# Spreads of 1/std on 32 rows of the array, in pairs, and paired second projection products

## The chip, the cores and the metric

The kernel runs on one core of one Trainium2 chip. The metric is the device time of one execution in microseconds. The engines are named as in the profile: PE is TensorE's matmul, PEld its loading of weights, DVE is VectorE, ACT is ScalarE, POOL is GpSimd, and SP, ACT and POOL issue DMAs. [...]

## The reference, cut to what matters

Four images of 96 channels and 64 x 64 pixels go through four residual layers: a bidirectional two-dimensional state space layer, a deformable convolution, a layer of Fourier mixing with a quantized feed-forward network, and linear attention with a second quantized feed-forward network. Two pieces matter here. The first is the layer normalization over channels, which stands ahead of the first layer, of the Fourier mixing, of the attention and of both feed-forward networks:

```python
def _ln_t(v, eps=1e-5):
    m = jnp.mean(v, axis=-1, keepdims=True)
    s = jnp.var(v, axis=-1, keepdims=True)
    return (v - m) / jnp.sqrt(s + eps)
```

The second is the projection ahead of the state space scan. It is taken over the pixels in row order and in column order (both also backwards):

```python
x0 = xc.reshape(Bsz, Di, L)
x1 = jnp.transpose(xc, (0, 1, 3, 2)).reshape(Bsz, Di, L)
x_hwwh = jnp.stack([x0, x1], axis=1)
xs = jnp.concatenate([x_hwwh, jnp.flip(x_hwwh, axis=-1)], axis=1)
x_dbl = jnp.einsum('bkdl,kcd->bkcl', xs, x_proj_w)
```

`Di` is 192, so each projection contracts over 128 + 64 channels.

## The kernel before, in words

**Layout.** Channels lie on partitions and pixels along the free dimension. An image of 4096 pixels is cut into 8 chunks of 512, the width of one PSUM bank.

**Norms.** `centred` multiplies each chunk by a centring matrix, squares the result on ScalarE, and sums the squares of all chunks of a norm into one bank: chunk j lands in the 32 partitions 32 (j % 4) and following, in row j // 4 of them. `inv_sqrt_steps` makes 1/std of that bank, one tile `rstd` of 128 x 512, in which the row 32 (j % 4) + j // 4 holds chunk j. To multiply a chunk by its 1/std, the row has to stand on all channel partitions. `spread` (line 523) does that: a matmul with `rstd` as the moving operand and one column of the identity, repeated 128 times, as weights. It writes one bank, `lnb` in the profile (`lnbf` in the feed-forward networks, `lnbo` in the output norm of the first layer). VectorE then multiplies the chunk by it (line 734 in the first layer, line 1613 in `normed`).

**Projection.** `projected` makes, for chunk j and each order q in `qs`, one bank `px`: first a product over 128 channels (line 812), then one over the last 64 (line 814), whose inputs lie on partitions 0 to 63 for row order and 64 to 127 for column order. ScalarE evicts the bank with a bias (line 815). Image 0 is projected one order at a time (`first`), images 1 to 3 with both orders in one call (`before`).

**The scan.** 1536 units of 128 x 1024 each. For each, ScalarE makes the decay (`da`, line 1014), TensorE spreads the inflow into two banks (`db`, line 1020), VectorE multiplies it (line 1034) and runs the recurrence (`hh`, line 1042), GpSimd weighs the states (line 1051), and TensorE sums them (`py`, line 1070). This is the frame of the kernel.

**Side work.** All else is two streams of Python generators that are stepped between the units: `ends` (image 0's start, the starts of images 1 to 3, then the last layers of each image) and `middle` (the output of the first layer and the deformable convolution of each image). A step issues a few instructions and yields their estimated cost. `pipe` runs several chains of steps at once and takes the next step that the planner's clock has room for. Every engine then runs its instructions in program order. After the last scan the side streams run alone; image 3's last layers run as two halves of the image.

**Banks.** While the scans run, both streams share three banks. `has_bank` tells whether one is free, by the count of banks held; a step says with `holds` how many its chain holds after it, and with `new` that the next step takes a new one. After the scans the `ends` stream, and the first half of image 3, has five banks of its own; the other stream keeps the three.

What the code before does at the places of the change:

```python
def chain(j):
    cs = slice(j * CH, (j + 1) * CH)
    pb = net.spread(rs, 32 * (j % 4) + groups.index(j // 4), C, key)
    yield cost(pe=1.2, holds=1)
    net.nc.vector.tensor_mul(tl[:C, cs], tl[:C, cs], pb)
    yield cost(dve=0.7)
```

Of the kernel before, what the change touches and what calls it, by code (L numbers as in the profile page):

```python
# [8 lines left out]
F32 = mybir.dt.float32  # L9
# [5 lines left out]
AF = mybir.ActivationFunctionType  # L15
# [4 lines left out]
B, C, H, W = 4, 96, 64, 64  # L20
# [5 lines left out]
CH = 512  # L26
NCH = L // CH
NR = CH // W
# [7 lines left out]
NX = 64 + R + 1 + 2 * NS  # L36
# [146 lines left out]
def cost(pe=0.0, dve=0.0, act=0.0, pool=0.0, **more):  # L183
    return Step((pe, dve, act, pool), **more)


def wait(us=0.0, **more):

    return Step((0.0,) * 4, us, **more)
# [82 lines left out]
def pipe(net, chains, width, every=0, lane=None, **tiles):  # L272


    chains, active = iter(chains), []
    clock, known, more = net.clock, net.known, True
    end, free = clock.now(), tiles
    while True:
        if more and len(active) < width:
            steps = next(chains, None)  # L280
            if steps is None:
                more = False
            else:
                active.append(Chain(steps, clock.now()))
                continue
        if not active:
            break
        for n, chain in enumerate(active):
            if chain.new and not net.has_bank():
                continue  # L290
            if any(
                a.done <= chain.done + every
                for a in active[:n]
                if lane is None or (a.kind is lane) == (chain.kind is lane)
            ):
                continue
            if not all(free[tag] > 0 for tag in chain.takes):
                continue
            if clock.has_room(known.get((chain.kind, chain.done), (1.0,) * 4), chain.ready):
                break  # L300
        else:
            yield BLOCKED
            continue
        for tag in chain.takes:
            free[tag] -= 1
        clock.precede(known.get((chain.kind, chain.done), (0.0,) * 4))
        step = next(chain.steps, None)
        if step is None:
            net.hold(-chain.holds)
            active.remove(chain)  # L310
            end = max(end, chain.ready)
            continue
        for tag in step.frees:
            free[tag] += 1
        known[chain.kind, chain.done] = step.work
        chain.ready = clock.queue(step, chain.ready)
        chain.done += 1
        net.hold(step.holds - chain.holds)
        chain.holds, chain.new, chain.takes = step.holds, step.new, step.takes
        yield None  # L320
    yield wait(max(0.0, end - clock.now()))
# [38 lines left out]
class Net:  # L360
# [39 lines left out]
        own = self.own_banks and self.stream.own  # L400
        return (self.own_banks if own else self.psum).tile([128, CH], F32, name=name, tag="mm")[:p]

    def has_bank(self):
        if self.own_banks:
            return self.stream.held < (5 if self.stream.own else 3)
        return sum(stream.held for stream in self.streams) < 3

    def hold(self, n):
        self.stream.held += n
# [63 lines left out]
    def centred(self, x, cen, dst, key, pool, bias=None, groups=(0, 1)):  # L473
# [36 lines left out]
        def chains():  # L510
            for r in groups:
                for q in range(4):
                    yield chain(4 * r + q)
                yield sums(r)

        yield from pipe(self, chains(), 5, every=-99, sq=4, v0=-3, v1=-3)
        rstd = pool.tile([128, CH], F32, name=f"lns{key}", tag="lns", bufs=1)
        nw = pool.tile([128, CH], F32, name=f"lnw{key}", tag="lnw", bufs=1)
# [4 lines left out]
    def spread(self, rstd, j, n, key):  # L523

        pb = self.mm(f"lnb{key}_{j}")
        row = self.ident[:, j : j + 1].to_broadcast([128, 128])
        self.nc.tensor.matmul(pb, lhsT=row, rhs=rstd, start=True, stop=True)
        return pb[:n]


# [24 lines left out]
class Layer0:  # L555
# [54 lines left out]
    def first(self):  # L610
# [5 lines left out]
        with tc.tile_pool(name=f"l0u{b}", bufs=1) as up, tc.tile_pool(name=f"l0b{b}", bufs=1) as sm:  # L616
# [25 lines left out]
            def columns():  # L642
                for j in range(NCH):
                    yield self.projected(b, j, us, xp_a, xp_c, sm, xdbl, (1,))
                    for ks in ((1,), (1, 3), (3,)):
                        yield self.steps(b, ks, j, us, dtw, sm, xdbl)

            yield from pipe(net, columns(), 5, every=2, ex=3, lw=2, rl=2, du=2)

    def before(self, b):  # L650
# [22 lines left out]
    @staticmethod  # L673
    def rows(pad, j):
        return pad[:, 1 + j * NR : 1 + (j + 1) * NR, 1 : 1 + W]

    @staticmethod
    def as_rows(t):
        return t.rearrange("p (h w) -> p h w", w=W)
# [25 lines left out]
    def normed_rows(self, b, x, pad):  # L705

        net, rows, as_rows = self.net, self.rows, self.as_rows
        tc, nc = net.tc, net.nc
        with tc.tile_pool(name=f"l0n{b}", bufs=2) as sm:
            for edge in (pad[:, 0, :], pad[:, PW - 1, :], pad[:, :, 0], pad[:, :, PW - 1]):  # L710
                nc.gpsimd.memset(edge, 0.0)
            yield wait(4.0)
            stats = []
            yield from net.group_norm_stats(x, sm, f"0_{b}", stats)
            mean, rstd = stats

            cen = sm.tile([C, 128], F32, name=f"cen{b}", tag="cen", bufs=1)
            nc.vector.tensor_scalar_mul(cen, net.cen96, rstd)
            yield cost(dve=0.3)
            net.hold(1)  # L720
            pb = net.mm(f"cb{b}")
            nc.tensor.matmul(pb[:, 0:1], lhsT=cen, rhs=mean, start=True, stop=True)
            bias = sm.tile([C, 1], F32, name=f"cenb{b}", tag="cenb", bufs=1)
            nc.scalar.mul(bias, pb[:C, 0:1], -1.0)
            net.hold(-1)
            yield cost(pe=0.3, act=0.3)

            rs = yield from net.centred(x, cen, lambda j: (rows(pad, j), as_rows), f"0_{b}", sm, bias)

            def chain(j):  # L730
                pb = net.spread(rs, 32 * (j % 4) + j // 4, C, f"0_{b}")
                yield cost(pe=1.2, holds=1)
                r = rows(pad, j)
                nc.vector.tensor_mul(r, r, as_rows(pb))
                yield cost(dve=0.7)
                nc.scalar.activation(r, r, AF.Identity, scale=net.vec(V_ING, C), bias=net.vec(V_INB, C))
                yield cost(act=0.8)

            yield from pipe(self.net, (chain(j) for j in range(NCH)), 3)

    def conv_weights(self, b, sm):

# [56 lines left out]
    def projected(self, b, j, us, xp_a, xp_c, sm, xdbl, qs, takes=""):  # L799


        net = self.net
        nc = net.nc
        cs = slice(j * CH, (j + 1) * CH)
        if takes:
            yield wait(new=True, takes=takes)
        for q in qs:
            xd = sm.tile([NX, CH], F32, name=f"xd{b}_{q}_{j}", tag=f"xd{q}")
            hp = slice(64 * q, 64 * q + 64)
            ua = us[0][:, cs] if q == 0 else us[1][:, j * NR : (j + 1) * NR, :]  # L810
            px = net.mm(f"px{b}_{q}_{j}")
            nc.tensor.matmul(px, lhsT=xp_a[:, q, :], rhs=ua, start=True, stop=False)
            yield cost(pe=1.3, holds=1)
            nc.tensor.matmul(px, lhsT=xp_c[hp], rhs=us[2][hp, cs], start=False, stop=True)
            nc.scalar.activation(xd, px[:NX], AF.Identity, bias=net.vec(V_X1, NX))
            xdbl[q, j] = xd
            yield cost(pe=1.3, act=0.7, new=q == 1 and len(qs) > 1)
        for q in qs:
            nc.sync.dma_start(self.bc_d[b][q][:, cs], xdbl[q, j][: 2 * NS])
            nc.sync.dma_start(self.bc_d[b][q + 2][:, cs], xdbl[q, j][64 + R + 1 :])  # L820
        yield NOTHING
# [781 lines left out]
def normed(net, t, tl, key, pool, groups=(0, 1)):  # L1603

    rs = yield from net.centred(
        t, net.cen96, lambda j: (tl[:C, j * CH : (j + 1) * CH], plain), key, pool, groups=groups
    )

    def chain(j):
        cs = slice(j * CH, (j + 1) * CH)  # L1610
        pb = net.spread(rs, 32 * (j % 4) + groups.index(j // 4), C, key)
        yield cost(pe=1.2, holds=1)
        net.nc.vector.tensor_mul(tl[:C, cs], tl[:C, cs], pb)
        yield cost(dve=0.7)

    yield from pipe(net, (chain(j) for j in chunks(groups)), 3)


def chunks(groups):
    return [4 * r + q for r in groups for q in range(4)]  # L1620


class Ffn:
# [23 lines left out]
    def run(self, b, t, groups=(0, 1), side="left"):  # L1647
# [3 lines left out]
        with (  # L1651
            tc.tile_pool(name=f"fb{n}_{b}", bufs=1, side=side) as big,
            tc.tile_pool(name=f"fs{n}_{b}", bufs=2, side=side) as pool,
        ):
            tl = big.tile([C, L], F32, name=f"fl{n}_{b}", tag="tl")
            yield from normed(net, t, tl, f"f{n}_{b}", pool, groups)

            def chunk(j):
# [49 lines left out]
class LinearAttention:  # L1708
# [8 lines left out]
    def run(self, b, t, groups=(0, 1), side="left", shared=None):  # L1717
# [3 lines left out]
        with (  # L1721
# [3 lines left out]
            tl = big.tile([C + 1, L], F32, name=f"tl3{key}", tag="tl")  # L1725
            nc.gpsimd.memset(tl[C:], 1.0)
            yield from normed(net, t, tl, f"3_{key}", pool, groups)
            net.hold(1)
            pa = net.mm(f"pa{key}", C)[:, :C]
# [191 lines left out]
```

## Time and profile before

| what | us |
|---|---|
| median of three runs | 8629.55 |
| lowest and highest of them | 8617.16, 8655.84 |
| the profiled execution, its own time | 8600.48 |
| its span, first to last instruction | 8598.7 |
| PE busy | 6553.4 |
| DVE busy | 6817.9 |
| ACT busy | 4945.4 |
| POOL busy | 5626.7 |

Durations are read from the one profiled execution. A busy TensorE is not TensorE at its peak, since matmuls are pipelined and their ends are modelled. An fp32 matmul shows as two matmul instructions, each with its own weight load. The groups that the change touches, from the page's list by line and engine (busy time, mean of one in ns, then the engine's idle time before them and what ended it):

```profile
L527 PE MATMUL lnb<-lns,w_ident 128*128 128x512 f32 x192 | 114.0, 726 | 23.4 <-DVE lns L436 14.2 <-issue 4.1 <-DVE tl L1613 3.6
L527 PE MATMUL lnbf<-lnsf,w_ident 128*128 128x512 f32 x128 | 74.4, 708 | 22.2 <-DVE lnsf L436 13.0 <-DVE fl L1613 9.2
L527 PE MATMUL lnbo<-rs,w_ident 128*128 128x512 f32 x64 | 51.4, 918 | 23.4 <-DVE rs L436 11.0 <-DVE cc L1173 5.0 <-DVE rl L853 4.4
L812 PE MATMUL px<-xa,w_xp_a 128*128 128x512 f32 x128 | 109.4, 947 | 41.1 <-DVE rl L853 24.8 <-DMA w_xp_a<-in_xp_a 8.9 <-ACT zt L789 7.0
L814 PE MATMUL px<-xc,w_xp_c 64*128 64x512 f32 x128 | 90.0, 790 | 0.0
```

### The profile page before, as it was taken

How to read it: one execution, taken by the hardware profiler on the slowest of the kernel's cores; microseconds unless marked ns; L12 is line 12 of the kernel's file. 1: busy time of each engine (PE TensorE's matmuls, PEld its weight loads, DVE VectorE, ACT ScalarE, POOL GpSimd, SP SyncE). 2: the span in 40 equal slices, each digit the busy share in tenths (PEclk: the TensorE clock that was granted, in tenths of full speed). 3: DMA queues.
4: the chain of work that ended last, by engine and by line, in shares of the span. 5: the costliest groups of instructions: out<-in, count | busy, mean ns of one | idle time of the engine just before them, and what ended most of it. 6: DMA issues, size and time to landing. Idle time of an engine off the chain costs nothing.

```text
span 8598.7 us, 97186 instructions
## 1 busy us (share of the span) xinstructions
PE 6553.4 (76%) x31960; PEld 2840.7 (33%) x31960; DVE 6817.9 (79%) x5118; ACT 4945.4 (58%) x9071; POOL 5626.7 (65%) x4308
## 2 busy tenths in 40 slices
PE   6775877689767668777767888777788776897587
PEld 2211221122222223311223555223455331464374
DVE  2799989888799888688898888888887887838714
ACT  5664666556567668755666667554567765333224
POOL 1565667566579788665688888665787886527700
PEclk8766877779677779876777888676788887798698
DMA  3677678868779889876888989766898887744420
GB/s 97 166 198 195 169 196 220 210 166 201 182 216 243 220 230 226 204 193 181 209 228 223 230 230 229 169 163 166 229 228 226 204 216 180 180 104 137 143 63 13
DMA packets 773932, 1608.32 MB, mean 187 GB/s; under 512 B 264081, under 2 KB 355757, under 8 KB 771222
## 3 DMA queue, kind: packets, MB, share of 16 engines
q10 hardware_dynamic: 244224, 843.17, 38.9%
q1 hardware_dynamic: 455478, 532.37, 24.0%
q0 software_dynamic: 73728, 226.57, 10.1%
q8 instruction: 256, 4.19, 0.2%
q14 instruction: 246, 2.02, 0.1%
HBM read 1345.43 MB, written 256.29 MB: 186 GB/s over the span
## 4 chain that ended last, share of the span: by engine, by line
PE 27%; DVE 14%; DMA 7%; ACT 7%; issue 4%; POOL 2%; ACTq 1%; SPq 1%; DVEq 0%; POOLq 0%
DVE hh L1042 7%; DVE db L1034 3%; PE ps L1416 3%; PE f L1510 3%; PE py L1070 3%; DMA da<-de 2%; PE pd L1432 2%; ACT g L1395 2%; PE db L1020 2%; ACT da L1014 1%; PE h L1551 1%; PE yp L1590 1%; PE zp L1576 1%; POOL hh L1051 1%; PE py L1065 1%
## 5 line engine op out<-in xcount | busy, mean ns | idle before, releaser
L1051 POOL TENSOR_TENSOR hh<-hh,bc 128x1024 f32<-128x1024 f32 x1536 | 3672.1, 2393 | 354.9 <-DVE hh L1042 225.1
L1042 DVE TENSOR_TENSOR_SCAN hh<-da,st,db 128x1024 f32<-128x1024 f32 x1152 | 2700.9, 2345 | 209.5 <-PE py L1070 79.8
L1034 DVE TENSOR_TENSOR db<-db,bc 128x1024 f32<-128x1024 f32 x1536 | 1864.0, 1214 | 610.2 <-PE db L1020 608.7
L1014 ACT ACTIVATE da<-da,w_al 128x1024 f32<-128x1024 f32 x1536 | 1737.6, 1146 | 476.8 <-DMA da<-de 129.9
L1383 POOL DMA_INDIRECT g<-table,idx x1152 | 1201.7, 1043 | 372.3 <-issue 174.8
L1020 PE MATMUL db<-du,rep 24*128 24x512 bf16 x3072 | 700.5, 457 | 780.1 <-DVE hh L1042 748.9
L1070 PE MATMUL py<-hh,w_fold 128*32 128x512 f32 x6144 | 1120.5, 792 | 35.4 <-POOL hh L1051 19.3
L1395 ACT ACTIVATE g<-g,wt 128x96 f32<-128x96 f32 x3456 | 968.3, 364 | 116.7 <-PE py L1070 30.7
L1042 DVE TENSOR_TENSOR_SCAN hh<-da,db 128x1024 f32<-128x1024 f32 x384 | 877.2, 2284 | 73.2 <-PE py L1070 25.1
L1416 PE MATMUL ps<-w_ident,g 128*96 128x128 f32 x3744 | 688.8, 329 | 222.8 <-issue 90.6
L1020 PEld LDWEIGHTS <-rep 24*128 24x128 bf16 x3072 | 159.5, 94 | 1909.3 <-issue 1228.5
L851 POOL TENSOR_TENSOR lw<-lw,w 128x512 f32<-128x512 f32 x192 | 244.0, 1271 | 718.0 <-DVE w L849 686.0
L1416 PEld LDWEIGHTS ps<-w_ident,g 128*96 128x96 f32 x3744 | 499.4, 148 | 568.6 <-ACT g L1395 176.7
L1049 POOL COPY st<-hh 128x1 f32<-128x1 f32 x1152 | 235.1, 204 | 685.3 <-DVE hh L1042 650.5
L763 PE MATMUL pc<-pad,wc 96*128 96x512 f32 x1152 | 568.7, 630 | 6.9 <-ACT st L1424 2.6
L1424 ACT COPY st<-ps 96x384 f32<-96x384 f32 x384 | 180.1, 472 | 543.6 <-PE ps L1416 506.0
L882 PE MATMUL pr<-ex,w_ident 128*128 128x512 f32 x384 | 294.7, 859 | 147.6 <-DVE ex L872 58.6
L840 PE MATMUL pd<-xd,w_dtw 103*64 103x512 f32 (+1 forms) x512 | 279.0, 820 | 68.1 <-DVE rl L853 30.4
L1432 PE MATMUL pd<-st,wdc 96*128 96x256 f32 x1152 | 320.5, 430 | 11.4 <-ACT st L1424 4.8
L763 PEld LDWEIGHTS pc<-pad,wc 96*128 96x128 f32 x1152 | 217.1, 199 | 308.7 <-issue 289.2
L1070 PEld LDWEIGHTS py<-hh,w_fold 128*32 128x32 f32 x6144 | 160.5, 125 | 387.4 <-issue 293.6
L1519 ACT COPY d<-f 128x512 f32<-128x512 f32 x192 | 111.2, 581 | 299.7 <-PE f L1510 287.5
(253 smaller groups left out, 8940.0 us busy)
## 6 DMA issues: line engine op xcount, KB each, us to landing
da<-de ACTq DMA_DIRECT2D x1536, 512.0 KB
du<-du SPq DMA_DIRECT2D x1536, 96.0 KB
bc<-bcd SPq DMA_DIRECT2D x128, 512.0 KB
y<-yb SPq DMA_DIRECT2D x384, 128.0 KB
de<-rl SPq DMA_DIRECT2D x128, 256.0 KB
m<-in_dft SPq DMA_DIRECT2D x128, 256.0 KB
ad<-y ACTq DMA_DIRECT2D x192, 128.0 KB
table<-pix SPq DMA_DIRECT2D x256, 96.0 KB
```

Source lines behind the costliest of these rows:

```text
L763: nc.tensor.matmul(pp, lhsT=wc[:, q, g * 128 : (g + 1) * 128], rhs=pad[:, r0 + dy : r0 + dy + NR, dx : dx + W], start=(q == 0), stop=(q == 8),
L882: nc.tensor.matmul(pr, lhsT=net.ident, rhs=ex, start=True, stop=False)
L1014: self.net.nc.scalar.activation(u.da, u.da, AF.Exp, scale=self.al[:, a : a + 1])
L1020: self.net.nc.tensor.matmul(db[:, h, :], lhsT=self.rep[64 * u.q + 32 * h : 64 * u.q + 32 * h + 24], rhs=u.du[64 * u.q + 32 * h : 64 * u.q ...
L1034: self.net.nc.vector.tensor_mul(u.db, u.db, u.bc[:, 0, :])
L1042: nc.vector.tensor_tensor_scan(u.along(u.hh), u.along(u.da), u.along(u.db), first, ALU.mult, ALU.add)
L1051: self.net.nc.gpsimd.tensor_mul(u.hh, u.hh, u.bc[:, 1, :])
L1070: nc.tensor.matmul(py[p0 : p0 + 32], lhsT=self.fold[:, u.i, :], rhs=hc[:, h * CH : (h + 1) * CH], start=u.sums["add"] is None and u.i == 0 ...
L1383: nc.gpsimd.indirect_dma_start(out=g[:, k, :], out_offset=None, in_=self.tables[b % 2], in_offset=bass.IndirectOffsetOnAxis(ap=idx[:, n : ...
L1395: nc.scalar.activation(pixel, pixel, AF.Identity, scale=wt[:, n, c : c + 1])
L1416: nc.tensor.matmul(pt[:, k, :], lhsT=g[:, k, c * C : (c + 1) * C], rhs=net.ident, is_transpose=True, start=(c == 0), stop=(c == corners - 1),)
L1432: nc.tensor.matmul(po, lhsT=wdc[:, k, :], rhs=st[:, k, :], start=(k == 0), stop=(k == 8))
```

## The change

`spread` takes only the 32 partitions that hold the wanted row, both of the identity's column and of `rstd`: the matmul contracts over 32 rows, and which 32 follows from the chunk. The two places that spread norms chunk by chunk (`normed_rows` and `normed`) now work on pairs of chunks: they ask for two banks, issue both spreads one after the other, and then multiply both chunks. `pipe` runs two such pairs at once instead of three single chunks. `gated`, which spreads the output norm, still issues one spread at a time.

In `projected`, a call with both orders asks for two banks, issues both first products, then both second products one after the other, then both evictions. `has_bank` takes the number of banks asked for.

```diff
-            if chain.new and not net.has_bank():
+            if chain.new and not net.has_bank(int(chain.new)):
...
-    def has_bank(self):
+    def has_bank(self, n=1):
         if self.own_banks:
-            return self.stream.held < (5 if self.stream.own else 3)
-        return sum(stream.held for stream in self.streams) < 3
+            return self.stream.held + n <= (5 if self.stream.own else 3)
+        return sum(stream.held for stream in self.streams) + n <= 3
...
         pb = self.mm(f"lnb{key}_{j}")
-        row = self.ident[:, j : j + 1].to_broadcast([128, 128])
-        self.nc.tensor.matmul(pb, lhsT=row, rhs=rstd, start=True, stop=True)
+        k = slice(j - j % 32, j - j % 32 + 32)
+        row = self.ident[k, j : j + 1].to_broadcast([32, 128])
+        self.nc.tensor.matmul(pb, lhsT=row, rhs=rstd[k], start=True, stop=True)
         return pb[:n]
...
-                pb = net.spread(rs, 32 * (j % 4) + j // 4, C, f"0_{b}")
-                yield cost(pe=1.2, holds=1)
...
-            yield from pipe(self.net, (chain(j) for j in range(NCH)), 3)
+                yield wait(new=2)
+                pbs = [net.spread(rs, 32 * ((j + i) % 4) + (j + i) // 4, C, f"0_{b}") for i in range(2)]
+                yield cost(pe=1.2, holds=2)
+                for i in range(2):
+                    r = rows(pad, j + i)
+                    nc.vector.tensor_mul(r, r, as_rows(pbs[i]))
+                    yield cost(dve=0.7, holds=1 - i)
+                    nc.scalar.activation(r, r, AF.Identity, scale=net.vec(V_ING, C), bias=net.vec(V_INB, C))
+                    yield cost(act=0.8, holds=1 - i)
+
+            yield from pipe(self.net, (chain(j) for j in range(0, NCH, 2)), 2)
...
-        if takes:
-            yield wait(new=True, takes=takes)
+        if takes or len(qs) > 1:
+            yield wait(new=len(qs), takes=takes)
+        pxs = {}
         for q in qs:
-            xd = sm.tile([NX, CH], F32, name=f"xd{b}_{q}_{j}", tag=f"xd{q}")
+            ua = us[0][:, cs] if q == 0 else us[1][:, j * NR : (j + 1) * NR, :]
+            pxs[q] = px = net.mm(f"px{b}_{q}_{j}")
+            nc.tensor.matmul(px, lhsT=xp_a[:, q, :], rhs=ua, start=True, stop=False)
+            yield cost(pe=1.3, holds=len(qs))
+        for q in qs:
             hp = slice(64 * q, 64 * q + 64)
...
-            yield cost(pe=1.3, act=0.7, new=q == 1 and len(qs) > 1)
+            nc.tensor.matmul(pxs[q], lhsT=xp_c[hp], rhs=us[2][hp, cs], start=False, stop=True)
+        for q in qs:
+            xd = xdbl[q, j] = sm.tile([NX, CH], F32, name=f"xd{b}_{q}_{j}", tag=f"xd{q}")
+            nc.scalar.activation(xd, pxs[q][:NX], AF.Identity, bias=net.vec(V_X1, NX))
+        yield cost(pe=1.3, act=0.7 * len(qs))
...
-    def chain(j):
-        cs = slice(j * CH, (j + 1) * CH)
-        pb = net.spread(rs, 32 * (j % 4) + groups.index(j // 4), C, key)
-        yield cost(pe=1.2, holds=1)
-        net.nc.vector.tensor_mul(tl[:C, cs], tl[:C, cs], pb)
-        yield cost(dve=0.7)
-
-    yield from pipe(net, (chain(j) for j in chunks(groups)), 3)
+    def chain(js):
+        yield wait(new=2)
+        pbs = [net.spread(rs, 32 * (j % 4) + groups.index(j // 4), C, key) for j in js]
+        yield cost(pe=1.2, holds=2)
+        for n, j in enumerate(js):
+            cs = slice(j * CH, (j + 1) * CH)
+            net.nc.vector.tensor_mul(tl[:C, cs], tl[:C, cs], pbs[n])
+            yield cost(dve=0.7, holds=1 - n)
+
+    js = chunks(groups)
+    yield from pipe(net, (chain(js[n : n + 2]) for n in range(0, len(js), 2)), 2)
```

More of the change, by code (lines that the diff above doesn't have):

```diff
@@ L730, in chain @@
             def chain(j):
-                pb = net.spread(rs, 32 * (j % 4) + j // 4, C, f"0_{b}")
-                yield cost(pe=1.2, holds=1)
-                r = rows(pad, j)
-                nc.vector.tensor_mul(r, r, as_rows(pb))
-                yield cost(dve=0.7)
-                nc.scalar.activation(r, r, AF.Identity, scale=net.vec(V_ING, C), bias=net.vec(V_INB, C))
-                yield cost(act=0.8)
-            yield from pipe(self.net, (chain(j) for j in range(NCH)), 3)
+                yield wait(new=2)
[8 more added lines that the diff above has]
+            yield from pipe(self.net, (chain(j) for j in range(0, NCH, 2)), 2)
     def conv_weights(self, b, sm):
@@ L804, in projected @@
         cs = slice(j * CH, (j + 1) * CH)
-        if takes:
-            yield wait(new=True, takes=takes)
+        if takes or len(qs) > 1:
+            yield wait(new=len(qs), takes=takes)
+        pxs = {}
         for q in qs:
-            xd = sm.tile([NX, CH], F32, name=f"xd{b}_{q}_{j}", tag=f"xd{q}")
-            hp = slice(64 * q, 64 * q + 64)
[L810 to L816, printed above, removed]
-            yield cost(pe=1.3, act=0.7, new=q == 1 and len(qs) > 1)
+            ua = us[0][:, cs] if q == 0 else us[1][:, j * NR : (j + 1) * NR, :]
[3 more added lines that the diff above has]
+        for q in qs:
+            hp = slice(64 * q, 64 * q + 64)
+            nc.tensor.matmul(pxs[q], lhsT=xp_c[hp], rhs=us[2][hp, cs], start=False, stop=True)
[3 more added lines that the diff above has]
+        yield cost(pe=1.3, act=0.7 * len(qs))
         for q in qs:
@@ L1607, in normed @@
     )
-    def chain(j):
-        cs = slice(j * CH, (j + 1) * CH)
-        pb = net.spread(rs, 32 * (j % 4) + groups.index(j // 4), C, key)
-        yield cost(pe=1.2, holds=1)
-        net.nc.vector.tensor_mul(tl[:C, cs], tl[:C, cs], pb)
-        yield cost(dve=0.7)
-    yield from pipe(net, (chain(j) for j in chunks(groups)), 3)
+    def chain(js):
[8 more added lines that the diff above has]
+    yield from pipe(net, (chain(js[n : n + 2]) for n in range(0, len(js), 2)), 2)
 def chunks(groups):
```

## The prediction

> **What bounds the kernel now.** I read the page first (busy shares, chain), then the busy times by stage, then VectorE's waits, then the timeline of a few places. The stages: before the first recurrence scan (0 to 185 us), while the 1536 scans run (185 to 7550), image 2's last layers beside image 3's sampling (7550 to 8180), image 3's layers alone (8180 to 8599).
>
> ```profile
> span 8598.7 us, 97186 instructions
> PE 6553.4 (76%) x31960; PEld 2840.7 (33%) x31960; DVE 6817.9 (79%) x5118; ACT 4945.4 (58%) x9071; POOL 5626.7 (65%) x4308
> PE 27%; DVE 14%; DMA 7%; ACT 7%; issue 4%; POOL 2%; ACTq 1%; SPq 1%; DVEq 0%; POOLq 0%
> ...
> 0.00:185.00 185.00, 121.12 (x264) 47.67 (x265) 33.77 (x63) 94.00 (x122) 9.04 (x15) 0.91 0.32 81
> 185.00:7550.00 7365.00, 5616.16 (x25948) 2243.70 (x25948) 6275.17 (x4295) 4531.98 (x8308) 5243.55 (x3980) 0.77 0.80 203
> 7550.00:8180.00 630.00, 455.20 (x2725) 295.88 (x2722) 374.71 (x534) 177.38 (x363) 366.61 (x311) 0.80 0.48 132
> 8180.00:8599.00 419.00, 360.88 (x3028) 253.44 (x3028) 134.27 (x228) 142.05 (x279) 7.45 (x2) 0.90 0.11 35
> ```
>
> The columns after the stretch are PE, PEld, DVE, ACT, POOL, then the granted clock. During the scans VectorE is busy for 6275 of 7365 us (85%) and TensorE for 5616 (76%): VectorE leads, and it is idle for 1090 us. In the last stage TensorE leads with 361 of 419 us.
>
> ```profile
> DVE db L1034 <- PE db L1020: 584.4, 278, 29.1
> DVE hh L1042 <- PE py L1070: 104.9, 98, 5.9
> ...
> DVE fl L1613 <- PE lnbf L527: 6.8, 4, 3.1
> ...
> DVE pad L734 <- PE lnb L527: 2.3, 2, 1.3
> ```
>
> These are VectorE's waits between 185 and 7550 us (total, times, longest). The multiplications that wait directly for a spread cost 9 us; 584 us are waits for `db`, the small product ahead of every scan, which stands in TensorE's queue behind whatever the side streams put there. With the smaller lines of that view (12.7, 12.7, 10.2, 7.3, 6.9, 6.8, 5.0, 2.6, 2.4, 2.3) VectorE waits for TensorE for 758 us in this stage. So TensorE time matters during the scans only as far as it delays `db`.
>
> **What the Trainium skill says.** "TensorE: Matmul & The Clock Gate", Part 3, says that matmuls in distinct 32-row groups run at the same time, and its closing table that one with 32 rows alone takes as long as one with 128. No spread here uses 32 rows, but two things agree. `db` has 24 rows, at partitions 32 apart, bf16: both start together. The fp32 `py` sums have 32 columns: eight instructions take 1.06 us.
>
> ```profile
> 5009.00 0.39 PE L1020 MATMUL db<-du,rep 24*128 24x512 bf16 x2
> 5009.31 1.06 PE L1070 MATMUL py<-hh,w_fold 128*32 128x512 f32 x8
> ```
>
> An fp32 product is two instructions, and at full clock one of 512 columns follows another every 0.43 us (weight loads of the first spreads at 58.24, 58.67 and 59.10 us). Eight in a row would be 3.4 us; in 1.06 us they ran four abreast, twice. For fp32 in row groups no line of this trace decides. "TensorEngine Tiling (Array Packing)", Key Properties, says that a change of tiling mode drains the engine, and its Gotcha 1 that row tiles must write different banks. The change gives each its own bank. The drain is visible: in the same place `o` at 5008.48 is followed by `db` after 0.52 us, not 0.43. I price a switch at 0.1 us.
>
> **The change, part by part.** The number of instructions of each kind on each engine is the same in both programs; 80 pairs of spreads stand directly behind each other on TensorE (head 4, scans 48, then 12 and 16), and 24 pairs of second projection products, all during the scans (images 1 to 3; image 0 projects one order at a time). The 32 spreads of the output norm (`lnbo`) keep their place and gain nothing.
>
> ```profile
> 0.00:185.00 185.00, 8.63 (x16) 3.61 (x16) 0.91 0.32 81
> 185.00:7550.00 7365.00, 164.59 (x252) 53.51 (x252) 0.77 0.80 203
> 7550.00:8180.00 630.00, 27.64 (x52) 9.85 (x52) 0.80 0.48 132
> 8180.00:8599.00 419.00, 38.97 (x64) 15.30 (x64) 0.90 0.11 35
> ```
>
> That is line 527, the spreads, by stage: PE and PEld busy, clock.
>
> Spreads during the scans: 164.6 us for 252 instructions; 60 are `lnbo` (51.4 us for 64 on the page's group, so 48 us), which leaves 116 us for 192 instructions, 48 pairs of 2.42 us. Side by side half remains, 1.21 us, plus two mode switches of 0.1: 1.0 us saved, 48 in all. If hi and lo parts cannot interleave, three steps of four remain: 0.4 us saved, 19 in all. Both ends are kept.
>
> Second projection products: 85.7 us for 122 instructions during the scans, 1.40 us a product, 24 pairs of 2.81 us. Side by side 1.40 us, and two of four switches go: 1.3 us net (I take 0.1 for imperfect overlap), 31 in all. The first products come back to back, their cost unchanged; both evictions (0.69 us each) come after the pair, on ScalarE at 62% busy: free.
>
> So TensorE loses 79 of 5616 us in this stage. How much of it reaches VectorE? Its side work is 5616 less `db` 699, `py` 1118 and 214 of line 1065: 3585 us, against 758 us of VectorE waits, 0.21 us of wait per us of side work. 79 x 0.21 = 17 us. From below it is nothing: a spread that was hidden stays hidden, and a TensorE with more pauses may be granted less clock (it has 0.77 now). From above I take 0.5, 40 us.
>
> Banks: the side streams share three during the scans, and a pair asks for two at once. The planner then holds the stream back, not the scan. In program order this does not happen on balance: nearly all VectorE side work of the changed program stands at the same scan or earlier (a few up to 6 later), by up to 42 scans between scans 430 and 960, because the planner books 1.2 us per pair where it booked 2.4; and it is back within a few scans at each point where a stream must wait for the scans themselves. Behind the last scan both programs hold the same 762 VectorE instructions. So nothing is moved into the end, and nothing out of it. New waits at a pair: its first multiplication starts some 0.1 to 0.2 us later, its second sooner; both stand in VectorE's order before a scan, cost below 0.2 x 48 = 10 us, against the second's gain; I take nothing.
>
> The end, image 3 alone: the spreads are on the path. At 8200.49 the sixteen take 9.65 us, and the last multiplication starts at 8210.17.
>
> ```profile
> 8200.49 9.65 PE L527 MATMUL lnb<-lns,w_ident 128*128 128x512 f32 x16 [4.17 <-DVE lns L436]
> ...
> 8210.17 0.68 DVE L1613 TENSOR_TENSOR tl<-tl,lnb 96x512 f32<-96x512 f32 x1 [0.17 <-PE lnb L527]
> ...
> 8211.00 2.27 PE L1551 MATMUL h<-w1e,tl 97*64 97x96 f32 x27 [0.87 <-DVE tl L1613]
> ```
>
> After the change the first multiplication still starts about 2.1 us in; then VectorE is the bound with eight of 0.70 us: over at 7.7 us instead of 10.4, 2.7 less. What is late next is VectorE. The two feed-forward norms, both halves interleaved, give some 2 us each, the two halves of the attention norm some 1 us each: 9 in all (5 if the clock stays low longer, 12 at most). Image 2's spreads (24, window 7550 to 8180) run beside image 3's sampling, whose indirect loads continue alone for 100 us after it: cover for most of it, I take 2 us (0 to 5). Head: the same eight as above on image 0's path, 2 us.
>
> Sum: 17 + 9 + 2 + 2 = 30 us. The profiled execution took 8600.48 us (span 8598.7), 29 less than the median 8629.55. 30 of 8600 is 0.35%; on the median that is 8600.
>
> **Rivals.** *The relief counts more (32%).* VectorE's waits are bursts (longest 29.1 us), and work cut from inside a burst counts fully; for: 278 waits carry 584 us. At 0.5, with 12, 5 and 2: 59 us, 8571. Against: spreads come in a stretch of few scans per norm, not everywhere. *No overlap of fp32 row groups (6%).* Then only the reordering remains: 8625 to 8630. For: the trace shows fp32 only across columns. Against: bf16 row groups do overlap. *Bunching (17%), slower.* With cheaper steps booked, the planner packs side work more densely behind `db` in scans 430 to 960; the mechanism is longer `db` waits there. For: the waits are uneven already (14.5 us of them between 708 and 1126 us, 75.5 between 7069 and 7550, 96 scans each: 0.15 and 0.79 us a scan). If 150 to 250 more scans get 0.4 us more, 60 to 100 us come back: 8660 to 8700; it decides once the `db` wait exceeds 584 by more than the 30 saved, and shows as slower past 43 us net. Against: the packed work is really shorter on TensorE, and the same total of VectorE work remains.
>
> **How the numbers follow.** Forecast 45%: 8600, its own range 8575 to 8625. The measurement of this kernel can tell about 0.5%, 43 us, from no change (its three runs lie 39 us apart): faster is below 8586, slower above 8673. The larger relief is nearly all faster, with a little of the forecast's low side: 0.36. Forecast, no overlap and the mild part of bunching are the same: 0.48. The rest, 0.16, is slower. Range 8545 to 8660.
>
> **What would show it.** Two spreads' instructions with equal starts, the pair of two at 0.9 us warm instead of 1.7; line 528 at about 24 + 48 us during the scans less than before (some 117 us in place of 165); the second products near 55 in place of 86 us; the first `h` after image 3's norm some 7.7 us after its first spread; the `db` wait near 565 us. I am wrong if starts are staggered, if the `db` wait grows, or if the stage of the scans moves by over 45 us.

## The result, and the profile after

The changed kernel takes 8625.84 us in the median of 20 runs (8604.64 to 8657.12), the kernel before 8638.25 (8610.36 to 8669.39). The ratio is 0.9985, with a 95% interval of 0.9972 to 0.9998: 12 us faster where 30 were forecast, and less than I had said a measurement could tell from no change. In two later measurements, on two chips, it was 0.9982 (0.9969 to 0.9996) and 0.9959 (0.9944 to 0.9974).

The two profiled executions are poor witnesses of the whole: that of the changed kernel took 8654.35 us, 28 above its median, that of before 8600.48, 38 below. So I read single steps from them, and whole stages only where several profiles agree.

The page's first lines, and the busy times by stage (head, scans, image 2's last layers beside image 3's sampling, image 3 alone; PE, PEld, DVE, ACT, POOL, then the clock):

```profile
span 8652.6 us, 97282 instructions
PE 6513.0 (75%) x31927; PEld 2842.9 (33%) x31960; DVE 6804.2 (79%) x5118; ACT 4941.9 (57%) x9071; POOL 5623.5 (65%) x4308
```

```profile
0.00:190.00 190.00, 125.07 (x263) 48.64 (x265) 32.97 (x62) 93.65 (x122) 9.04 (x15) 0.87 0.31 80
190.00:7576.00 7386.00, 5571.81 (x25944) 2238.82 (x25975) 6263.76 (x4296) 4530.46 (x8309) 5239.09 (x3981) 0.76 0.79 202
7576.00:8240.00 664.00, 473.34 (x2692) 309.00 (x2692) 374.83 (x533) 176.11 (x361) 368.04 (x311) 0.74 0.43 123
8240.00:8652.00 412.00, 342.81 (x3028) 246.43 (x3028) 132.61 (x228) 141.65 (x279) 7.37 (x2) 0.88 0.12 39
```

The clock is lower than before in every stage of this profile (0.91, 0.77, 0.80 and 0.90 there). Beside the sampling that is no sign of the 32 rows: a profile of the new order with 128 rows has 0.76 in that stage too (`pairs_128rows_again`, below). The clock's records in the profiles hold only two values, 1 and 0.5, full and half clock; a number between them is a mean over time. The products do what the change says. A pair in the timeline of TensorE at 1803 us (of the two instructions in a row of `lnb`, one belongs to each spread):

```profile
1803.18 0.70 PE L528 MATMUL lnb<-lns,w_ident 32*128 32x512 f32 x2 [2.18 <-DVE pad L737]
1803.20 0.39 PE L1025 MATMUL db<-du,rep 24*128 24x512 bf16 x2
1803.71 0.78 PE L528 MATMUL lnb<-lns,w_ident 32*128 32x512 f32 x2
```

The first parts of both spreads start together, the second parts 0.53 us later, and the `db` products slip in between. fp32 products in different row groups overlap, which the trace of before could not decide. The spreads, line 528, by stage (PE and PEld busy, clock), and below them the second projection products, line 818, during the scans:

```profile
0.00:190.00 190.00, 7.19 (x16) 2.93 (x16) 0.87 0.31 80
190.00:7576.00 7386.00, 147.65 (x252) 41.41 (x252) 0.76 0.79 202
7576.00:8240.00 664.00, 18.31 (x52) 4.87 (x52) 0.74 0.43 123
8240.00:8652.00 412.00, 20.55 (x64) 6.48 (x64) 0.88 0.12 39
...
190.00:7576.00 7386.00, 52.30 (x122) 13.53 (x122) 0.76 0.79 202
```

The second products fell from 85.7 to 52.3 us, as worked out. In image 3's own layers the spreads fell from 39.0 to 20.6 us. During the scans they fell by 17 us only, from 164.6, where 48 were forecast. VectorE's waits for TensorE from 190 to 7576 us:

```profile
DVE db L1039 <- PE db L1025: 582.8, 259, 25.9
DVE hh L1047 <- PE py L1075: 104.2, 90, 4.9
```

This window begins ahead of the wait for the first `db`, 25.9 us; the one of the kernel before, with 584.4 us, began behind it. Counted alike, without it, the changed kernel has 556.9 us, and 539.1 and 553.9 in two more profiles. So the wait for `db` did shrink, by 28 to 45 us, near the 565 forecast; the wait for `py` did not (104.9 before). And image 3's norm in the last layers:

```profile
8264.82 5.49 PE L528 MATMUL lnb<-lns,w_ident 32*128 32x512 f32 x16 [4.16 <-DVE lns L436]
...
8266.31 4.87 DVE L1620 TENSOR_TENSOR tl<-tl,lnb 96x512 f32<-96x512 f32 x8 [1.63 <-PE lnb L528]
...
8271.32 8.99 PE L1556 MATMUL h<-w1e,tl 97*64 97x96 f32 x115 [1.01 <-DVE tl L1620]
```

VectorE's eight multiplications now run without a gap and are the bound, and `h` starts 6.5 us after the first spread; before it was 10.5.

### The profile page after: what moved, and what is told of

It reads as the page before. It is cut to its first block, busy times and chain, and to the rows that moved or that the text cites. A ratio compares the mean times of both kernels' runs of the same rounds, so it can differ in the third digit from the quotient of the medians.

```text
span 8652.6 us, 97282 instructions
## 1 busy us (share of the span) xinstructions
PE 6513.0 (75%) x31927; PEld 2842.9 (33%) x31960; DVE 6804.2 (79%) x5118; ACT 4941.9 (57%) x9071; POOL 5623.5 (65%) x4308
## 4 chain that ended last, share of the span: by engine, by line
PE 36%; DVE 29%; DMA 11%; ACT 9%; issue 8%; POOL 4%; SPq 2%; ACTq 1%; DVEq 0%; another core or an unknown queue 0%; POOLq 0%
DVE hh L1047 14%; DVE db L1039 7%; PE py L1075 4%; PE pc L766 4%; PE ps L1421 4%; PE f L1515 3%; DMA da<-de 3%; PE pd L1437 3%; ACT g L1400 2%; PE db L1025 2%; POOL hh L1056 2%; ACT da L1019 2%; DMA m<-in_dft 1%; PE py L1070 1%; DMA du<-du 1%
```

## The experiments

All kernels compute the whole reference. Ratios are to the kernel before on the same chip; the kernels did not all run on one chip, and from chip to chip the ratio of the same kernel moved by up to 0.0027, some 23 us (0.9924 and 0.9951 for `projection_alone`). The clock is the mean over a kernel's runs; before has 0.782 to 0.785, the changed kernel 0.771 to 0.773. The last column is the granted clock 4 to 8 us after the start of a spread, averaged over all spreads during the scans of one profile.

| kernel | spreads | projection | ratio (95% interval) | clock | after a spread |
|---|---|---|---|---|---|
| before | 128 rows, single | single | 1 | 0.785 | 0.86 |
| changed | 32, pairs | pair | 0.9985 (0.9972 to 0.9998) | 0.771 | 0.57 |
| pairs_128rows | 128, pairs | pair | 0.9934 (0.9916 to 0.9953) | 0.787 | 0.86 |
| rows32_single | 32, single | single | 1.0039 (1.0023 to 1.0056) | 0.765 | 0.62 |
| projection_alone | 128, single | pair | 0.9924 (0.9893 to 0.9954) | 0.788 | 0.86 |
| spreads_alone | 32, pairs | single | 0.9978 (0.9966 to 0.9991) | 0.770 | 0.59 |
| rows64_pairs | 64, pairs | pair | 0.9960 (0.9943 to 0.9978) | 0.779 | 0.66 |
| rows64_single | 64, single | single | 1.0015 (1.0002 to 1.0029) | 0.776 | 0.70 |
| pairs128_alone | 128, pairs | single | 0.9977 (0.9961 to 0.9992) | 0.786 | 0.86 |
| rows32_single_proj | 32, single | pair | 0.9981 (0.9965 to 0.9997) | 0.773 | 0.58 |

**The parts.** Two kernels change only the rows of the spread and keep every engine's program order: `pairs_128rows` has the order of the changed kernel, `rows32_single` that of the kernel before. The edit of the first (the second is its reverse, made in the kernel before):

```diff
-        k = slice(j - j % 32, j - j % 32 + 32)
-        row = self.ident[k, j : j + 1].to_broadcast([32, 128])
-        self.nc.tensor.matmul(pb, lhsT=row, rhs=rstd[k], start=True, stop=True)
+        row = self.ident[:, j : j + 1].to_broadcast([128, 128])
+        self.nc.tensor.matmul(pb, lhsT=row, rhs=rstd, start=True, stop=True)
```

> The changed kernel with spreads over all 128 rows: every engine's program order is that of the changed kernel, only the overlap of the spreads is gone (that of the second projection products stays). Theory A (the relief of TensorE is what counts, the order costs nothing): the projections alone are left, ratio to the kernel before about 0.999, 5 to 10 us faster. Theory B (the overlap gains some 25 us, the new order and the asking for two banks at once give 10 to 15 back): slower than the kernel before by 5 to 15 us, ratio 1.0005 to 1.002, and slower than the changed kernel by 20 to 25 us. Theory C (TensorE's relief is lost to a lower granted clock): equal to the changed kernel within 5 us, with a clock above 0.771.

> The kernel before with spreads of 32 rows, one chunk at a time: every engine's program order is that of the kernel before. 93 of its 192 spreads stand directly ahead of another one, so many can overlap without pairs. Theory A: a part of the gain, 5 to 15 us faster than before, no better than the changed kernel. Theory B: more than the changed kernel gains, 15 to 25 us faster than before, ratio 0.997 to 0.998. Theory C: nothing, ratio 0.999 to 1.001.

Both came out on the far side of all three theories. Without the overlap, on another chip, the changed kernel gains four times as much (0.9934), and 32 rows in the old order lose 34 us (1.0039). In both orders it is the 32 rows that cost, and the clock goes with them. The other two take one part of the change each, `has_bank(n)` included:

> The paired second projection products alone (with the count of banks asked for). Theory A: 31 of the 79 us that I took off TensorE during the scans, at 0.21 us each: 5 to 8 us faster. Theory B: the order moves as well, 5 us faster to 10 us slower. Theory C: nothing, and line 818 still at 52 to 60 us in place of 86.

> The paired spreads on 32 rows alone. Theory A: 20 to 25 us faster, ratio 0.997 to 0.998, image 3's own layers some 11 us shorter, the stage of the scans 5 to 10 us shorter. Theory B: 5 to 15 us faster, with the stage of the scans or the stage after it, where image 2's last layers and image 3's sampling share the engines, not shorter than before. Theory C: only the 11 us of image 3's own layers.

The projection, priced at 5 to 8 us, gave 66. The spreads gave 19, but with the low clock. The parts, measured on one chip, do not add up to the whole, which gave 12 to 32 in its three measurements.

**64 rows, and the missing corners.** From here theory D is that TensorE's clock follows how much of the array is used. `rows64_pairs` pairs chunks j and j + 2, so that two spreads fill all rows:

```diff
-        k = slice(j - j % 32, j - j % 32 + 32)
-        row = self.ident[k, j : j + 1].to_broadcast([32, 128])
+        k = slice(j - j % 64, j - j % 64 + 64)
+        row = self.ident[k, j : j + 1].to_broadcast([64, 128])
...
-    yield from pipe(net, (chain(js[n : n + 2]) for n in range(0, len(js), 2)), 2)
+    yield from pipe(net, (chain(js[n : n + 3 : 2]) for m in range(0, len(js), 4) for n in (m, m + 1)), 2)
```

> The changed kernel with spreads of 64 rows, chunks j and j + 2 as a pair, so that the two together fill all 128 rows. Theory D (TensorE's granted clock follows how much of the array a stretch uses; the 32-row spreads let it fall to about 0.6 for some 15 us at every norm, which costs more than their overlap gains): the clock around the spreads stays at 0.75 or more, mean clock 0.78 to 0.79, and the kernel is at least as fast as pairs_128rows, 55 to 85 us faster than before, ratio 0.990 to 0.994. Theory B (the loss lies in the overlap itself or in the order): like the changed kernel, ratio 0.997 to 1.000.

> The kernel before with spreads of 64 rows, one chunk at a time, in the program order of before. Theory D: between before and rows32_single, which ran at a ratio of 1.0039: 1.000 to 1.003, mean clock 0.765 to 0.785. If only a step at 32 rows counts: 0.998 to 1.000 and the clock of before.

> Paired spreads over 128 rows, projection as before: the program order of spreads_alone (0.9978 with 32 rows). Theory D: faster than spreads_alone by some 30 to 45 us, as in the other two pairs of kernels of equal order, ratio 0.992 to 0.995, mean clock 0.785 or more. Theory B: slower than spreads_alone, 1.000 to 1.003.

> The paired projection products with spreads of 32 rows, one at a time: the program order of projection_alone (0.9924). Theory D: 30 to 45 us slower than projection_alone, ratio 0.996 to 0.998, mean clock about 0.765. Theory B: 5 to 15 us faster than projection_alone.

The order of the clocks is that of the rows: about 0.86 after a spread with 128, 0.66 to 0.70 with 64, 0.57 to 0.62 with 32. But 64-row pairs, which fill the array together, do not hold it, so that part of D is wrong: it is the rows of each product that go with the clock, not the sum of a pair. The overlap does not make it: the output norm's spreads stand alone, and after them the clock is 0.77 to 0.81 in three profiles of `pairs_128rows` and 0.54 to 0.55 in three of the changed kernel. Nor is it that TensorE was busy for less of the time: with `rows64_single` it was busy for 0.80 of the first 4 us from a spread's start and 0.82 of the next 4, before the change for 0.79 and 0.74. How the clock is set stays open.

`pairs128_alone` is a miss too: 0.9977, no better than `spreads_alone` with the same order (0.9978 on another chip), although its clock is higher (0.786 against 0.770). `rows64_single` lies where D put it, and `rows32_single_proj` close to it (0.9981 where 0.996 to 0.998 was expected, and a clock of 0.773).

**On one chip.**

> The changed kernel once more, on one chip with pairs_128rows_again. Theory D (32-row spreads cost TensorE's clock): ratio 0.997 to 1.000 and mean clock about 0.770 over its runs, 0.3 to 0.6% above pairs_128rows_again. Theory B (order or overlap; the earlier difference between the two was one of chips): within 0.2% of it.

> The program order of the changed kernel with 128-row spreads. Theory D: ratio 0.992 to 0.995, mean clock about 0.787, and the clock in the first microseconds after a spread at 0.8 or more, against 0.6 in after_again.

0.9982 (0.9969 to 0.9996) against 0.9928 (0.9908 to 0.9949): medians of 8581.63 and 8535.42 us, 46 us for the rows alone, as D said. Their profiles show where. First, 20 us from the start of the spreads of the same four norms in either program (stretch, busy times, clock), the changed kernel:

```profile
921.00:941.00 20.00, 13.25 (x36) 3.00 (x40) 19.76 (x16) 9.07 (x11) 10.15 (x8) 0.50 0.45 119
4532.00:4552.00 20.00, 17.53 (x67) 5.98 (x64) 17.12 (x14) 12.66 (x32) 17.16 (x16) 0.52 0.89 232
6832.00:6852.00 20.00, 16.75 (x83) 8.71 (x82) 17.06 (x14) 13.50 (x33) 18.00 (x16) 0.76 0.71 194
7060.00:7080.00 20.00, 15.48 (x56) 6.10 (x56) 18.16 (x15) 11.49 (x31) 16.08 (x13) 0.66 0.86 209
```

and with 128 rows:

```profile
911.00:931.00 20.00, 12.43 (x32) 3.83 (x32) 19.76 (x16) 8.96 (x11) 10.17 (x8) 0.84 0.44 119
4492.00:4512.00 20.00, 15.84 (x56) 6.34 (x58) 15.93 (x13) 12.20 (x31) 14.10 (x14) 0.67 0.89 226
6783.00:6803.00 20.00, 18.40 (x90) 9.18 (x90) 19.28 (x15) 12.72 (x32) 17.89 (x17) 0.95 0.80 221
7007.00:7027.00 20.00, 16.73 (x64) 7.40 (x63) 18.94 (x15) 11.56 (x30) 16.86 (x13) 0.84 0.86 209
```

At these four the clock is 0.15 to 0.34 lower; over the 29 places of the scans where both programs begin a norm's spreads with the same one, it is lower at 26. The spreads' own durations say the same (minimum, median and maximum in ns), 32 rows first, from each kernel's list of line 528 or 527:

```profile
L528 PE MATMUL lnb<-lns,w_ident x192: 587/1056/1218, 55.3 to 8494.9; 32*128 32x512 f32 x192
```

```profile
L527 PE MATMUL lnb<-lns,w_ident x192: 590/593/1223, 54.7 to 8441.2; 128*128 128x512 f32 x192
```

At full clock the two forms take the same 0.59 us; the median 32-row spread ran at half clock. Over the scans, the whole stage, and then line 528 or 527 in it, with 32 rows:

```profile
189.70:7533.00 7343.30, 5568.14 (x25944) 2235.75 (x25975) 6267.19 (x4295) 4531.31 (x8309) 5242.27 (x3980) 0.76 0.80 204
...
189.70:7533.00 7343.30, 146.67 (x252) 41.55 (x252) 0.76 0.80 204
```

and with 128:

```profile
184.60:7469.70 7285.10, 5516.53 (x25944) 2222.51 (x25975) 6263.03 (x4295) 4528.77 (x8309) 5238.78 (x3980) 0.78 0.81 205
...
184.60:7469.70 7285.10, 168.00 (x252) 55.02 (x252) 0.78 0.81 205
```

The spreads save 21 us of TensorE, and yet TensorE is busy 52 us longer: most of the rest on it runs slower (in the mean, `db` takes 461 ns against 454 and `py` 804 against 794). The stage is 58 us longer, and VectorE's wait for `db` is larger, 32 rows first:

```profile
DVE db L1039 <- PE db L1025: 564.4, 272, 25.3
```

```profile
DVE db L1038 <- PE db L1024: 531.0, 258, 25.4
```

As the order is the same, the time from one scan to the next can be compared scan by scan. Over three profiles of either kernel the scans take 61 us longer with 32 rows. 22 of these fall in the 171 scans from three before to five after a paired spread, 12 in 117 around an output norm's (whose single spreads gain nothing), 27 in the 1247 others. In the first two groups each of the three profiles with 32 rows is longer than each of those with 128; in the last they mix. So a loss is located at the spreads, and the rest is not told from noise. All of it stands in VectorE's waits for TensorE: summed over the scans they are 748, 720 and 752 us with 32 rows, 687, 658 and 693 with 128, a difference of 61 in the mean (before, 759).

The same profiles tell what goes with the clock where the program is the same. Between the three profiles of one kernel, a stretch of 16 scans takes 0.28 us (changed kernel) or 0.22 us (`pairs_128rows`) longer for each us more that it spends at half clock. The 32 rows put 287 us more of the scans at half clock. At that rate this is an estimated 62 to 81 us, enough for the 61 measured. It is a relation between executions; no run sets the clock by itself.

The projection was taken apart next. `proj_full` keeps the order of `projection_alone` but takes the second products of images 1 to 3 over all 128 rows, with zero weights in the half of the other order; nothing overlaps:

```diff
+    z = np.zeros_like(xpp[0, 128:])
+    a["xp_c"] = c(np.stack([np.concatenate([xpp[0, 128:], z]), np.concatenate([z, xpp[1, 128:]])], axis=1))
...
-            hp = slice(64 * q, 64 * q + 64)
-            nc.tensor.matmul(pxs[q], lhsT=xp_c[hp], rhs=us[2][hp, cs], start=False, stop=True)
+            hp = slice(0, 128) if len(qs) > 1 else slice(64 * q, 64 * q + 64)
+            nc.tensor.matmul(pxs[q], lhsT=xp_c[hp, q, :], rhs=us[2][hp, cs], start=False, stop=True)
```

> The paired projection products alone, once more, as the base for proj_full on the same chip. If the first measurement holds: ratio 0.990 to 0.995. My priced gain was 5 to 8 us, 0.999.

> projection_alone with the second products of images 1 to 3 over all 128 rows, with zero weights in the half that belongs to the other order: same program order on every engine but for the weight's load, no overlap. Theory E (the gain of the projection part comes from the order, in which the planner sets side work earlier): ratio within 0.2% of projection_alone_again. Theory F (it comes from the overlap and the fuller array): back to 0.998 to 1.002.

0.9951 (0.9930 to 0.9973) with the overlap, 0.9947 (0.9928 to 0.9967) without. The gain, some 35 to 42 us here, is the program order's; the overlap adds nothing that can be measured. The intervals reach some 18 us to either side, so the 5 to 8 us that I had priced for it are neither shown nor excluded.

**What in the order, and a better kernel.** `booking_only` is the kernel before with the second products of images 1 to 3 booked at half; `proj_booked` is `projection_alone` with the pair booked at twice:

```diff
-            yield cost(pe=1.3, act=0.7, new=q == 1 and len(qs) > 1)
+            yield cost(pe=0.65 if len(qs) > 1 else 1.3, act=0.7, new=q == 1 and len(qs) > 1)
```

```diff
-        yield cost(pe=1.3, act=0.7 * len(qs))
+        yield cost(pe=1.3 * len(qs), act=0.7 * len(qs))
```

> The kernel before; the projections of images 1 to 3 are issued as before, but their two second products are booked at 0.65 us each in place of 1.3, so that the planner's total is that of the changed kernel. Theory E1 (the booking makes the gain): 0.994 to 0.997. Theory E2 (the arrangement of the products makes it: both first ones, both second ones, then both evictions, with two banks asked for): 0.999 to 1.002.

> projection_alone with its pair of second products booked at 2.6 us, so that the planner's total is that of the kernel before. VectorE's side work then stands within a few scans of its place before. E1: 0.999 to 1.002. E2: 0.994 to 0.997, as projection_alone and proj_full.

0.9984 (0.9969 to 0.9998) and 0.9988 (0.9973 to 1.0003): either alone gives little, 19 and 13 us by the medians, with intervals of some 13 us to either side. Their sum is near the 35 us of both together on the other chip, so they may simply add up. What in the order makes the gain stays open. `hybrid` is `rows64_pairs` with 64 rows only after the scans:

```diff
-        k = slice(j - j % 64, j - j % 64 + 64)
-        row = self.ident[k, j : j + 1].to_broadcast([64, 128])
+        n_rows = 64 if self.own_banks else 128
+        k = slice(j - j % n_rows, j - j % n_rows + n_rows)
+        row = self.ident[k, j : j + 1].to_broadcast([n_rows, 128])
```

> Pairs everywhere and the paired projection; spreads over 128 rows while the scans run, over 64 rows (chunks j and j + 2, side by side) once the streams have banks of their own. Theory D with the overlap that the last layers showed (image 3's own layers 409.7 us with 64-row pairs against 424.3 with 128 rows, in one profile each): 10 to 15 us faster than pairs_128rows_third, ratio about 0.991, mean clock 0.785 or more. If the lower clock costs as much there as it gains: equal to it.

> The base for hybrid on the same chip: 0.992 to 0.995, mean clock about 0.787, as twice before.

`hybrid` has 0.9916 (0.9887 to 0.9945) with a clock of 0.789, its base 0.9931 (0.9905 to 0.9956): medians of 8529.90 and 8545.93 us. The 16 us lie just above the 10 to 15 expected, but the intervals overlap, and in the profiles image 3's own layers give 9 of them (412.3 against 421.7 us). `hybrid` is faster than the kernel before (79 us on that chip), and by its ratio than the changed one, which ran on other chips.

**Work added to hold the clock.** `filled` writes a 128-row spread into each bank ahead of the 32-row one:

```diff
+        full = self.ident[:, j : j + 1].to_broadcast([128, 128])
+        self.nc.tensor.matmul(pb, lhsT=full, rhs=rstd, start=True, stop=True)
         self.nc.tensor.matmul(pb, lhsT=row, rhs=rstd[k], start=True, stop=True)
```

> The changed kernel in which a 128-row spread of the same row is written into each bank ahead of the 32-row one: 192 more products on TensorE (0.86 us each at full clock, 165 us in all), the same result. Theory D (the clock falls because the 32-row products use a quarter of the array): the clock around the spreads stays at 0.75 or more, mean clock 0.78 or more, and the kernel is faster than after_third by 10 to 40 us in spite of the added work. If the 32-row form costs by itself (drains between tiling modes, the start of the pair), the added work comes on top: 15 to 50 us slower than after_third.

> The changed kernel on the chip of filled, as its base: 0.997 to 0.9995, mean clock about 0.771.

The clock 4 to 8 us after a spread came back to 0.74 from 0.58, but the time rose to 1.0288 (1.0243 to 1.0332), 282 us above `after_third`. I had mispriced it: 192 full spreads at the 1.19 us that one costs in the page of before (114.0 us for 96) are 228 us, and they stand between the two spreads of a pair, so those no longer overlap. As a test of time it says nothing. It does show that the added work lifts the clock at the same places; but TensorE was also busy for 0.95 of the first 4 us from a spread's start, in place of 0.76, so full rows and denser work are not told apart here.

## Why the prediction was wrong

The sum was 30 us, the measured gain 12 to 16 in two measurements and 32 in a third. That the third meets the sum, and that the time lies in the range of 8545 to 8660, is luck: the reasons don't hold.

- *Overlap of fp32 row groups:* right. The rival without overlap fell, and so did the one in which the relief counts more: the gain is 12 to 32 us, not 59. The price of a switch of tiling mode was right too: in the profile of before, at full clock, `db` starts 0.52 us after an fp32 instruction of 128 x 512 (the median of 139), the next fp32 one of 128 rows 0.43 us after it.
- *Second products, 31 us off TensorE:* right in size, 33. But 0.21 us of VectorE per us of TensorE was not seen for it: `proj_full`, without the overlap, is as fast, within some 18 us.
- *Spreads, 48 us off TensorE during the scans:* 17 in the first profile, 21 in the comparison of equal orders, because most pairs ran at half clock. I had halved a measured 2.42 us without asking whether the clock would stay.
- *"From below it is nothing: [...] a TensorE with more pauses may be granted less clock":* this is the step that failed. I named the clock and bounded its harm at zero. In equal order, on one chip, the 32 rows cost 46 us net of all they save; in the old order, 34. That this is the clock rather than some other cost of the form rests on four things: the clock falls at the spreads more than elsewhere, other TensorE work takes longer, the loss lies at the spreads, and the rate at which a program loses time at half clock covers it. Two switches of 0.09 us at each of the 126 spreads of the scans would be some 23 us of TensorE, and that passed on at 0.21 only 5 us (an estimate). One pair of equal orders (`spreads_alone`, `pairs128_alone`) shows the clock without the loss; it stands on two chips, whose difference may hide a part. So the link from clock to time is well supported, but not isolated.
- *VectorE's wait for `db`, near 565 us:* it came, 557, 539 and 554, but not by the relief alone: with 128 rows in the same order, where the spreads give no relief, the waits for TensorE are shorter still.
- *The order, "nothing is moved into the end, and nothing out of it", taken at zero:* wrong the other way. `pairs_128rows`, the new order with the spreads' overlap undone, is 0.7% faster, 57 to 63 us by the medians on three chips. Where the work stands behind the last scan was a poor measure; the scans themselves are shorter (7365.6 us in the profile of before; 7324.7, 7285.1 and 7312.3 in three profiles of `pairs_128rows`). Bunching, the rival that was to be slower through longer `db` waits, named the order with the wrong sign.
- *Image 3's own layers, 9 us:* right, 425.7 us before, 414.2, 413.2 and 417.4 after; with the new order and 128 rows 424.3, 421.5 and 421.7.
- *The stage beside image 3's sampling, 2 us:* can't be read; it varies from 605 to 673 us over the profiles.
- *Head, 2 us faster:* wrong, 185.0 us to the first scan before, 190.5, 189.7 and 189.9 after, at a clock of 0.87 in place of 0.91. With 128 rows in the same order it is 181.3, 184.6 and 181.6.

So a small net gain came out as the difference of two terms, on the chip where both ran 62 us gained by the order (with the second products' overlap, whose own gain was not measurable) and 46 us lost with the rows, neither of which stood in my sum.

## What to carry to other kernels

Before a full-array product is cut into row groups, look at what runs beside it: a lower clock for everything around it can cost more than the overlap gains. Here row groups lost time during the scans, where TensorE was busy for 76% of the time, and gained it in image 3's own layers, where the spreads were on the path and TensorE was busy for 86%. Where a planner orders the work, separate the order from the instruction: run the new order with the old form, and the old order with the new form. A booked cost is part of the change, even where the real work is the same.

## What was not expected of the hardware

A few narrow products move the mean clock of a whole execution: 192 spreads of 32 rows, 384 of some 31960 matmul instructions, took it from 0.788 to 0.773 on one chip. The clock 4 to 8 us after a spread was 0.86 with 128 rows, 0.66 to 0.70 with 64, and 0.57 to 0.62 with 32; two 64-row products side by side were no better than single ones. "TensorE: Matmul & The Clock Gate", Part 1, in the Trainium skill says that the gate follows how busy TensorE is; in these runs the rows of a product count too. And the two parts of an fp32 product interleave with those of its neighbour in another row group, so that a pair takes two steps, not three.
